# Two attention layers over four images in float32: the last image's output projection by seven half products

## The chip, the cores and the metric

The kernel runs on one core of a Trainium2 chip. The metric is the time of one execution on the device in microseconds, as the median of several runs. A separate execution was recorded by the hardware profiler; all names of engines below are the profile's: PE is TensorE's matmuls and PEld its weight loads, DVE is VectorE, ACT is ScalarE, POOL is GpSimd, and SP is SyncE, which here only issues transfers. An engine carries out its instructions in the order in which the program emitted them.

## The reference

The input x has 4 images of 32 x 32 positions with 768 channels, all in float32. Two layers follow one another. Each layer normalises x over 32 groups of channels, computes attention with 12 heads of 64 channels over the 1024 positions of an image, with a bias from relative positions in the scores, projects the result and adds it to x:

```
x = x + attention_0(groupnorm(x)) @ Wproj_0 + bproj_0
x = x + attention_1(groupnorm(x)) @ Wproj_1.T + bproj_1
attention: softmax(scale * q k^T + rel_h + rel_w) v,   q, k, v = projections of groupnorm(x)
```

The change is in the last line's projection, for the last image of the second layer: an output of 768 channels by 1024 positions from the attention's 768 channels.

## The kernel before

**Units of work.** A layer of one input image is called an image here: images 0 to 3 are layer 0, 4 to 7 layer 1; image 7 is the last (`LAST`). An image has six pairs of heads (`pair` 0 to 5, each 128 channels), a pair has eight units (`n` 0 to 7, each 128 query positions). One loop (L1005) goes over all 384 units, and its body writes the order of the instructions of every engine out by hand, a unit at a time, under a manual schedule. In each unit the body emits: transfers and other things due at the start; two bias additions on GpSimd for the unit after next (`biases`, L528); the score matmuls of the next unit (`scores`, L543); their softmax up to the exponentials on VectorE and ScalarE (`exponentials`, L556); the transposes of this unit's weights on VectorE and their store to DRAM (`turn`, L578: td<-tb), read back later in another layout (`read_back`, L587: pt<-td); the reciprocal on VectorE and the two divisions on ScalarE for the next unit (`divide`, L571); sums on GpSimd that are due; and then pieces of projections. At n = 6 and n = 2 it emits the attention-times-values matmuls (`weigh`, L598), 64 instructions, whose result VectorE evicts from PSUM into `attn` tiles (L622).

**The bias from positions.** For each pair, part of the bias goes through DRAM: ScalarE stores it (tdr<-t), and four transfers on SP read it back along diagonals (rel<-tdr, L521). The bias additions of units 4 to 7 wait for the second set.

**Projections by seven products.** The products of a pair (q, k, v) and the output projections of images 0 to 6 are computed by a scheme of the Strassen-Winograd kind: the matrices are split in two along the contracted channels, the outputs and the positions, and seven products of halves with some sums replace eight. For the output projection these are called a (two products), b (two), c (two) and d (one), for o = 0, 1, 2, each with contracted pairs 0 to 2 in one half and 3 to 5 in the other (`out_product`, L711). The differences of weights that they need are made beforehand by GpSimd and kept in DRAM tables (`combined`, L628; `single`, L650: for layer 1, in images 3 and 4). The sums of attention tiles are made on GpSimd (`out_sums`, L698). VectorE evicts the products. Kind a needs pairs 0 to 2 alone and runs in pairs 4 and 5 of the image; b, c and d need the others too and run in pairs 0 to 3 of the next image.

**The last image** has no next one. Its projection is plain (`project_out_two`, L821; `project_out`, L829; `put_result`, L842): for each of 6 output chunks and 2 halves of positions, six contracted pairs, in the three parts that `CUTS` (L624) tells: pairs 0 to 2, pairs 3 and 4, pair 5. That is 72 matmuls of 128 x 128 by 128 x 512. The first part for outputs 0 and 1 runs in pair 4 and at the start of pair 5 in the form called crossed: matmuls of 64 rows, two at a time on the two halves of the array, the product begun in one unit and finished in a later one. The rest is a list `todo`, from which `take` (L900) emits as many matmuls at the end of each unit of the last pair as `shares` tells: 3, 6, 0, 6, 6, 6, 0, 6, then 24. After that come the last attention-times-values matmuls and the last six products (L1137).

**Evictions and buffers.** Products go to PSUM tiles of the pool `ps_m`, which has two buffers (L79); attention-times-values and the position matmuls use the same two. A product begins when the tile before last has been evicted. The eviction of a product is emitted with its last matmul, that is behind that unit's transposes, reciprocal and divisions. `put_result` adds the first part to the residual and the output's bias on VectorE (L846), the other parts to that sum (L849). The residual halves and the weights are loaded by `fetch` (L792) and `fetch_last` (L808) on SP's queue. Most 128 x 512 tiles come from one pool of 35 shared buffers (`unit`, L89, `UNITS`, L54).

Of the kernel before, what the change touches and what calls it, by code (L numbers as in the profile page):

```python
# [57 lines left out]
def attention_blocks(ctx: ExitStack, tc: tile.TileContext, a: dict, out: bass.AP):  # L58
# [539 lines left out]
    def weigh(g, quarters):  # L598

        if quarters[0] % 2 == 0:
            attn_of.setdefault(g, []).append(unit(f"attn_{g}_{quarters[0] // 2}"))
        n = len(quarters)
        av = ps_m.tile([P, S], FP, tag="m", name=f"av_{g}_{quarters[0]}")[:, : n * 2 * P]
        for at, quarter in enumerate(quarters):
            for k in range(NT):
                for h in range(2):
                    rows = slice(h * D, (h + 1) * D)  # L610
                    nc.tensor.matmul(  # L611
                        av[rows, at * 2 * P : (at + 1) * 2 * P], lhsT=v_of[g][:, k, rows],
                        rhs=pt_of[g, quarter].rearrange("p n r k h i -> p (n r) k h i")[:, :, k, h, :],
                        start=(k == 0), stop=(k == NT - 1),
                    )
        at = quarters[0] % 2 * 2 * P
        to = attn_of[g][quarters[0] // 2][:, at : at + n * 2 * P]
        im, pair = divmod(g, NP)
        if images[im][0] == 0:
            nc.vector.tensor_copy(to, av)  # L620
        else:
            nc.vector.tensor_scalar(to, av, bqkv[:, 2, pair : pair + 1], None, ALU.add)  # L622

    CUTS = [0, NC // 2, NC - 1, NC]  # L624
    LAST = NI - 1
    tables = {}
# [23 lines left out]
    def single(l, o, which):  # L650

        if (l, o) not in tables:
            tables[l, o] = dram.tile([4, P, NB * P], FP, tag=f"tw{l}_{o}", name=f"tw_{l}_{o}")
        raw = lambda k: a[f"wo{l}"][o + k % 2 * NB][:, k // 2 * NB * P : (k // 2 + 1) * NB * P]
        made = lambda k: tables[l, o][k - 1]
        x, y = (unit(f"t{k}_{l}_{o}_{which}")[:, : NB * P] for k in range(2))
        for to, at in zip((x, y), {
            1: lambda: (raw(1), raw(0)), 2: lambda: (raw(3), made(1)),
            4: lambda: (raw(2), made(2)), 3: lambda: (raw(3), raw(1)),
        }[which]()):  # L660
            nc.sync.dma_start(out=to, in_=at)
        at_sums.setdefault(here[0] + 2, []).append(
            lambda: nc.gpsimd.tensor_tensor(x, x, y, ALU.subtract)
        )
        at_start.setdefault(here[0] + 3, []).append(
            lambda: nc.sync.dma_start(out=made(which), in_=x)
        )
# [9 lines left out]
    def fetch_out(at):  # L677

        if at >= len(order):
            if at < len(order) + 2:  # L680
                fetch(3 + 4 * (at - len(order)))
            return
# [13 lines left out]
    s3_of, kept_x, kept_y = {}, {}, {}  # L696

    def out_sums(im, which, c):  # L698

        part = lambda k, i: attn_of[im * NP + k * NB + c][i]  # L700
        if which == 3:
            s3_of[im, c] = unit(f"os3_{im}_{c}")
        to, x, y, op = {
            3: lambda: (s3_of[im, c], part(0, 0), part(0, 1), ALU.subtract),
            1: lambda: (part(0, 1), part(0, 1), part(1, 1), ALU.add),
            2: lambda: (part(0, 0), part(0, 1), part(0, 0), ALU.subtract),
            4: lambda: (part(1, 0), part(1, 0), part(0, 0), ALU.subtract),
        }[which]()
        nc.gpsimd.tensor_tensor(to, x, y, op)

    def out_product(im, kind, o):  # L711
        l = images[im][0]
        ws = out_weights[im, kind, o]
        half = lambda p, i: [attn_of[im * NP + p * NB + c][i] for c in range(NB)]
        t = ps_m.tile([P, 2, HALF], FP, tag="m", name=f"o{kind}_{im}_{o}")
        if kind == "d":
            for c in range(NB):
                for h, rows in enumerate(ROWS):
                    nc.tensor.matmul(  # L719
                        t[:, h, :], lhsT=ws[0][rows, c, :], rhs=half(1, 0)[c][rows],  # L720
                        start=(c == 0), stop=(c == NB - 1),
                    )
        else:
            xs = {
                "a": lambda: (half(0, 0), [s3_of[im, c] for c in range(NB)]),
                "b": lambda: (half(1, 0), half(0, 0)),
                "c": lambda: (half(0, 1), half(1, 1)),
            }[kind]()
            yield from crossed(t, range(NB), lambda t, c, h, rows: (
                t[:, h, :], ws[h][rows, c, :], xs[h][c][rows]  # L730
            ))
        t0, t1 = t[:, 0, :], t[:, 1, :]
# [5 lines left out]
        if kind == "a":  # L738
            kept_x[o], kept_y[o] = unit(f"ox_{im}_{o}"), unit(f"oy_{im}_{o}")
            nc.vector.tensor_copy(kept_x[o], t0)  # L740
            add(kept_y[o], t1, kept_x[o])
        elif kind == "b":
# [3 lines left out]
            add(y, t1, y)  # L746
# [8 lines left out]
        else:  # L755
            x = kept_x[o]
            with_bias(x, t0, x, o + NB)
            add(x, t1, x)
            complete(im, o + NB, 0, x, (3, 6, 14)[o])
        at = order_of[im, kind, o]  # L760
        ahead_by = {"d0": (2, 3), "c2": (3,), "d1": (), "d2": (2,)}
        for k in ahead_by.get(f"{kind}{o}", (2,)):
            early.append(lambda k=k: fetch_out(at + k))

    def complete(im, o, i, r, delay):
        l, b = images[im]
        if im + 1 == LAST and delay > 4:
            delay = 2
# [19 lines left out]
    parts = [(o, i) for o in range(NC) for i in range(2)]  # L788
    res_of, sum_of = {}, {}
    fetched = [0, 0]  # L790

    def fetch(upto):  # L792

        l, b = images[LAST]
        while fetched[0] <= min(upto, len(parts) - 1):
            o, i = parts[fetched[0]]
            if i == 0:
                w = wopool.tile([P, NB, P], FP, tag="wo", name=f"wo_{LAST}_{o}")
                nc.sync.dma_start(
                    out=w, in_=a[f"wo{l}"][o][:, : NB * P].rearrange("p (c o) -> p c o", o=P)  # L800
                )
                for c in range(NB):
                    wo_of[LAST, o, c] = w[:, c, :]
            res_of[o, i] = unit(f"res_{LAST}_{o}_{i}")
            load_half(res_of[o, i], l, b, o, i)
            fetched[0] += 1

    def fetch_last():  # L808
# [3 lines left out]
        for c in range(NC // 2, NC):  # L812
            if c + 1 < NC:
                w = weights_of(NPAIR, "ac"[c - NC // 2])
# [6 lines left out]
    def project_out_two(o):  # L821
        t = ps_m.tile([P, 2, HALF], FP, tag="m", name=f"oo_{o}")
        yield from crossed(t, range(NB), lambda t, c, i, rows: (
            t[:, i, :], wo_of[LAST, o, c][rows], attn_of[LAST * NP + c][i][rows],
        ))
        for i in range(2):
            put_result(0, o, i, t[:, i, :])

    def project_out(p, o, i):  # L829
        c0, c1 = CUTS[p : p + 2]  # L830
        t = ps_m.tile([P, S], FP, tag="m", name=f"o_{p}_{o}_{i}")[:, :HALF]
        for c in range(c0, c1):
            nc.tensor.matmul(  # L833
                t, lhsT=wo_of[LAST, o, c], rhs=attn_of[LAST * NP + c][i],
                start=(c == c0), stop=(c == c1 - 1),
            )
            if c < c1 - 1:
                yield True
        put_result(p, o, i, t)
        yield True  # L840

    def put_result(p, o, i, t):  # L842
        l, b = images[LAST]
        if p == 0:
            sum_of[o, i] = to = res_of[o, i]
            nc.vector.scalar_tensor_tensor(to, t, bo[l][:, o : o + 1], to, ALU.add, ALU.add)  # L846
        else:
            to = sum_of[o, i]
            nc.vector.tensor_tensor(to, t, to, ALU.add)  # L849
        if p == 2:  # L850
            nc.sync.dma_start(out=chunk(dsts[l][b], o)[:, i * HALF : (i + 1) * HALF], in_=to)
        if p == 0 and i == 1:
            fetch(2 * o + 9)
# [24 lines left out]
    def out_groups(g):  # L878
# [3 lines left out]
        if im == LAST and pair >= 4:  # L882
            make = [lambda o=o: project_out_two(o) for o in range(2)] if pair == 4 else [None, None]
        else:
            at = im if pair >= 4 else im - 1
            if at < 0:
                return {}
            make = [
                (lambda name=name: out_product(at, name[0], int(name[1]))) if name else None
                for name in plan if name is not None  # L890
            ]
# [5 lines left out]
    def put_out(p, groups):  # L897
        return [(project_out(p, at // 2, at % 2), CUTS[p + 1] - CUTS[p]) for at in groups]
# [27 lines left out]
    for k in range(NB):  # L926
        for stage, after in enumerate((0, 4, 5, 6)):
            combining.setdefault(NT * k + after, []).append((0, k, stage))
    singles = [(0, 3), (1, 3), (2, 3), (0, 1), (0, 2), (0, 4), (1, 1), (1, 2), (2, 1), (2, 2), (1, 4), (2, 4)]
    singles = {  # L930
        ((3 + k // 6) * NP + p) * NT + n: made
        for k, (made, (p, n)) in enumerate(zip(singles, 2 * [(0, 1), (0, 4), (1, 2), (2, 4), (3, 2), (4, 0)]))
# [15 lines left out]
    with tc.manual_schedule(engines=ENGINES):  # L948
# [56 lines left out]
        for at, (g, n) in enumerate(units):  # L1005
# [3 lines left out]
            if n == 0:  # L1009
# [10 lines left out]
                if g + 1 == NPAIR:  # L1020
                    fetch_last()
                    todo = put_out(0, range(4, 12)) + put_out(1, range(12))
                    todo += put_out(2, range(0, 12, 2))
# [81 lines left out]
            if not end:  # L1105
                for which, c in sum_steps.get((pair, n), ()):
                    sums(im + 1, which, c)
            if (pair, n) in out_sum_steps:
# [17 lines left out]
            take(todo, shares[n])  # L1126
            if n == 6:
# [9 lines left out]
        todo = put_out(2, range(1, 12, 2))  # L1137
# [56 lines left out]
```

## Time and profile before

| | us |
|---|---|
| median of three runs | 3244.69 |
| lowest, highest | 3243.01, 3245.06 |
| profiled execution, its own time | 3248.18 |
| its span, first to last instruction | 3246.2 |
| images 1 to 6, from first score matmul to first score matmul | 398.8 to 400.3 |
| last pair, scores of unit 1 to the last attention-times-values matmuls | 3155.56 to 3229.05 |

Times in the profile count from the span's first instruction. A float32 matmul appears as two instructions. Matmuls overlap in the array, so that starts, not durations, tell their pace. In a timeline, equal instructions that follow one another are one line (x12 is twelve of them), and the bracket at its end tells how long the engine was idle before it and what ended that. A row of the groups gives the line, the engine, what is written from what, the number of instructions, their busy time and the mean ns of one, and then the idle time before them.

### The profile page before, as it was taken

Reading aid. Unit: us, or ns where it says so; the run is one execution under the profiler, and the core shown is the slowest. Engines: PE = TensorE matmul, PEld = TensorE weight load, DVE = VectorE, ACT = ScalarE, POOL = GpSimd, SP = SyncE. Lnnn points to the kernel's source line nnn. Section 1 sums busy time; section 2 is a strip of 40 time slices with the busy share of each in tenths; the row PEclk is TensorE's granted clock in tenths of the full one; section 3 lists DMA queues with packets and bytes.
Section 4 is the critical chain, followed back from the end, with each engine's and each line's share of the span. In section 5 each row is a group of like instructions: output and inputs, shape, how many; then the busy total and the mean of one; then the engine's idle time right before and its main releaser. Section 6 shows DMA issues by size and latency. Waiting matters only on the chain.

```text
span 3246.2 us, 63998 instructions
## 1 busy us (share of the span) xinstructions
PE 3216.8 (99%) x24800; PEld 1855.4 (57%) x24800; DVE 2578.6 (79%) x4085; ACT 2093.2 (64%) x3098; POOL 2571.3 (79%) x1364
## 2 busy tenths in 40 slices
PE   8999999999999999999999999999999999999999
PEld 5565555555565555555565555555565555555554
DVE  7888878887888877788777887778777788787785
ACT  5677766666566665667656676666766567665662
POOL 6888967789777897878978889777897778977762
PEclk9999999999999999999999999999999999999999
DMA  5998888999989998899988999789988899888996
GB/s 196 339 340 320 311 310 313 323 338 327 319 303 330 342 328 317 296 346 343 324 308 309 342 338 339 284 302 335 325 325 302 298 340 330 312 311 303 322 337 252
DMA packets 386847, 1028.84 MB, mean 317 GB/s; under 512 B 31344, under 2 KB 73200, under 8 KB 337392
## 3 DMA queue, kind: packets, MB, share of 16 engines
q1 hardware_dynamic: 370992, 997.33, 86.2%
q10 hardware_dynamic: 15552, 27.43, 2.3%
q8 instruction: 196, 3.21, 0.4%
q14 instruction: 107, 0.88, 0.1%
HBM read 566.93 MB, written 457.70 MB: 316 GB/s over the span
## 4 chain that ended last, share of the span: by engine, by line
PE 94%; DVE 3%; DMA 2%; issue 1%; ACT 0%; POOL 0%; SPq 0%; DVEq 0%; POOLq 0%
PE pj L357 22%; PE av L611 20%; PE s L550 20%; PE pv L357 11%; PE pj L385 4%; PE oa L357 3%; PE ob L357 3%; PE oc L357 3%; PE tp L488 2%; PE pv L441 2%; PE od L719 2%; PE o L833 1%; DMA td<-tb 1%; DVE tb L582 1%; DMA pt<-td 1%
## 5 line engine op out<-in xcount | busy, mean ns | idle before, releaser
L536 POOL TENSOR_TENSOR sc<-rel 128x1024 f32<-128x1024 f32 x768 | 1943.6, 2557 | 537.8 <-DVE tb L582 416.0
L576 ACT ACTIVATE sc<-sc,sm 128x1024 f32<-128x1024 f32 x768 | 841.1, 1143 | 595.0 <-DVE sm L573 481.3
L562 DVE CUSTOM_DVE_ANT_0 sc<-s,sc 128x1024 f32<-128x1024 f32 x768 | 911.3, 1226 | 337.5 <-PE s L550 323.5
L566 ACT ACTIVATE sc<-sc,sm 128x1024 f32<-128x1024 f32 x768 | 877.2, 1144 | 255.7 <-DVE sm L562 253.2
L582 DVE STREAM_TRANSPOSE tb<-sc 128x1024 f32<-128x1024 f32 x768 | 912.4, 1233 | 18.3 <-DMA td<-tb 17.1
L550 PE MATMUL s<-k,q 64*128 64x512 f32 x3072 | 736.4, 596 | 0.5 <-DVE k L401 0.5
L611 PE MATMUL av<-pt,v 128*64 128x256 f32 x6144 | 684.9, 381 | 5.1 <-DMA pt<-td 5.1
L611 PEld LDWEIGHTS av<-pt,v 128*64 128x64 f32 x6144 | 433.7, 137 | 285.5 <-issue 42.8
L550 PEld LDWEIGHTS s<-k,q 64*128 64x128 f32 x3072 | 285.0, 187 | 296.6 <-issue 264.3
L357 PEld LDWEIGHTS pv<-wv,xn 64*128 64x128 f32 x4608 | 271.3, 188 | 35.1 <-issue 28.9
L357 PE MATMUL pv<-wv,xn 64*128 64x128 f32 x4608 | 273.8, 272 | 0.5 <-DVE wv L346 0.5
L357 PE MATMUL pj<-xn,wa 64*128 64x512 f32 x1152 | 265.6, 593 | 4.2 <-DVE wa L346 2.6
L357 PE MATMUL pj<-xn,w 64*128 64x512 f32 x1152 | 263.2, 589 | 0.0
L357 PE MATMUL pj<-s,w 64*128 64x512 f32 x576 | 262.9, 590 | 0.0
L357 PE MATMUL pj<-s,wc 64*128 64x512 f32 x576 | 262.9, 590 | 0.0
L357 PEld LDWEIGHTS pj<-xn,wa 64*128 64x128 f32 x1152 | 111.0, 187 | 140.9 <-issue 115.5
L357 PEld LDWEIGHTS pj<-xn,w 64*128 64x128 f32 x1152 | 111.7, 187 | 135.5 <-issue 133.1
L459 DVE TENSOR_TENSOR v<-pv,v 128x512 f32<-128x512 f32 x216 | 140.2, 686 | 57.9 <-ACT v L461 40.9
L493 ACT COPY t<-tp 128x512 f32<-128x512 f32 x96 | 56.1, 585 | 160.6 <-PE tp L488 160.6
L511 ACT COPY rel<-raw 32x256 f32<-32x256 f32 x384 | 154.8, 403 | 3.6
L357 PEld LDWEIGHTS pv<-wv,s 64*128 64x128 f32 x2304 | 137.1, 188 | 24.2 <-issue 16.9
L357 PEld LDWEIGHTS pj<-s,wc 64*128 64x128 f32 x576 | 105.6, 187 | 68.6 <-issue 64.8
(134 smaller groups left out, 3395.8 us busy)
## 6 DMA issues: line engine op xcount, KB each, us to landing
td<-tb SPq DMA_DIRECT2D x384, 1024.0 KB, 5.3
pt<-td SPq DMA_DIRECT2D x382, 1024.0 KB, 8.3
tdr<-t ACTq DMA_DIRECT2D x96, 256.0 KB, 5.4
wa<-in_wqk SPq DMA_DIRECT2D x48, 384.0 KB, 4.2
wc<-in_wqk SPq DMA_DIRECT2D x48, 384.0 KB, 5.6
wv<-in_wv SPq DMA_DIRECT2D x24, 768.0 KB, 11.8
xn<-in_x SPq DMA_DIRECT2D x48, 256.0 KB, 5.4
res<-in_x SPq DMA_DIRECT2D x48, 256.0 KB, 5.7
```

The lines of the kernel that those rows point to most:

```text
L357: nc.tensor.matmul(to, lhsT=w, rhs=x, start=at == half == 0, stop=at == 0 and half == 1)
L385: nc.tensor.matmul(t[:, h, :], lhsT=w[rows, c, :], rhs=x[c][rows, :], start=(c == 0), stop=(c == NB - 1),)
L441: nc.tensor.matmul(t[:, h, b, :], lhsT=s4[c][rows, b * P : (b + 1) * P], rhs=w22[rows, c, :], start=(b, c) == (0, 0), stop=(b, c) == (3, N ...
L459: add = lambda to, x, y: nc.vector.tensor_tensor(to, x, y, ALU.add)
L511: nc.scalar.copy(rel[rows], raw[rows, :, :, WIDE - 1 - HW - y : WIDE - 1 - y])
L536: nc.gpsimd.tensor_tensor(sc.rearrange("p (a k) (u l) -> p a (k u) l", a=4, l=8), rel[:, h, m, :].unsqueeze(1).unsqueeze(3).to_broadcast(s ...
L550: nc.tensor.matmul(ps[h][:, cols], lhsT=q[rows, n * P : (n + 1) * P], rhs=k[rows, cols], start=True, stop=True,)
L562: nc.vector.tensor_tensor_reduce(out=sc, in0=ps[h], in1=sc, scale=-scale, scalar=BIG, op0=ALU.add, op1=ALU.min, accum_out=st[:, 0, h : h + 1],
L566: nc.scalar.activation(sc, sc, AF.Exp, bias=st[:, 0, h : h + 1], scale=-1.0, accum_out=st[:, 1, h : h + 1],)
L576: nc.scalar.mul(sc, sc, st[:, 2, h : h + 1])
L582: nc.vector.transpose(tb[:, :, h, :], sc_of[g, n, h])
L611: nc.tensor.matmul(av[rows, at * 2 * P : (at + 1) * 2 * P], lhsT=v_of[g][:, k, rows], rhs=pt_of[g, quarter].rearrange("p n r k h i -> p (n ...
```

## The change

For the last image, pairs 0 to 3 are projected by seven half products as in the other images, with two pairs in each half (`width` is 2 in place of 3); pairs 4 and 5 are added afterwards in the plain form, each on its own.

- a0 and a1 run in crossed form where the plain products of outputs 0 and 1 ran. The other products (a2, b0 to b2, c0, c1, d0, d1, c2, d2) are at the head of `todo`, as full matmuls of 128 rows, four for a, b and c and two for d (`last_product`); then come twelve products of one matmul each for pair 4, and six for pair 5. The shares are as before.
- Both results of an a are copied out of PSUM by ScalarE; the sum that VectorE made there is now made by GpSimd when b is evicted. The residual is added by GpSimd (`add_last`, a unit later where there is one), and pairs 4 and 5 are added to that by VectorE.
- `weigh` evicts the first values of the last pair (pair 5's unit 6) on ScalarE in place of VectorE.
- The differences of weights for two pairs are made in images 5 and 6, as those for three pairs are in images 3 and 4: twelve times two loads, a GpSimd subtraction and a store.
- Sums of attention tiles run on GpSimd in pair 4 (`last_sums`), one a unit, and two at once in unit 4 of pair 5.
- Weights of the products are loaded into shared buffers, two transfers of 128 KB each, from unit 2 of pair 4 on (`last_fetches`); the residual halves in units 1 to 6 of the last pair, two a unit (`load_last`); `fetch_last` loads two weight tiles in place of three.

```diff
+        if g + 1 == NPAIR and n == 2:
+            nc.scalar.activation(to, av, AF.Identity, bias=bqkv[:, 2, pair : pair + 1])
+        elif images[im][0] == 0:
...
+    width = lambda im: NB if im < LAST else NB - 1
...
+    last_order = ("a0", "a1", "a2", "b0", "b1", "b2", "c0", "c1", "d0", "d1", "c2", "d2")
...
+    def last_product(kind, o):
+        ws, xs = out_operands(LAST, kind, o)
+        n = width(LAST)
+        t = ps_m.tile([P, 2, HALF], FP, tag="m", name=f"o{kind}_{LAST}_{o}")
+        for h, (w, x) in enumerate(zip(ws, xs)):
+            for c in range(n):
+                nc.tensor.matmul(
+                    t[:, h, :], lhsT=w[:, c, :], rhs=x[c], start=(c == 0), stop=(c == n - 1)
+                )
+                if (h, c) < (len(ws) - 1, n - 1):
+                    yield True
+        out_results(LAST, kind, o, t, [t[:, h, :] for h in range(len(ws))])
+        yield True
...
         if kind == "a":
             kept_x[o], kept_y[o] = unit(f"ox_{im}_{o}"), unit(f"oy_{im}_{o}")
+            if im == LAST:
+                nc.scalar.copy(kept_x[o], t0)
+                nc.scalar.copy(kept_y[o], t1)
+                return
             nc.vector.tensor_copy(kept_x[o], t0)
             add(kept_y[o], t1, kept_x[o])
         elif kind == "b":
             x, y, r = kept_x[o], kept_y[o], unit(f"or_{im}_{o}_0")
             with_bias(r, t0, x, o)
             add(x, t1, x)
-            add(y, t1, y)
+            if im == LAST:
+                nc.gpsimd.tensor_tensor(y, y, x, ALU.add)
+            else:
+                add(y, t1, y)
...
+            if len(ts) == 2:
+                add(x, t1, x)
...
     def complete(im, o, i, r, delay):
         l, b = images[im]
+        if im == LAST:
+            sum_of[o, i] = r
+            add_last = lambda: nc.gpsimd.tensor_tensor(r, r, res_of[o, i], ALU.add)
+            if here[0] + 1 < len(units):
+                at_sums.setdefault(here[0] + 1, []).append(add_last)
+            else:
+                add_last()
+            return
...
+    def project_out(c, o, i):
+        t = ps_m.tile([P, S], FP, tag="m", name=f"o_{c}_{o}_{i}")[:, :HALF]
+        nc.tensor.matmul(
+            t, lhsT=wo_of[LAST, o, c], rhs=attn_of[LAST * NP + c][i], start=True, stop=True
+        )
+        to = sum_of[o, i]
+        nc.vector.tensor_tensor(to, t, to, ALU.add)
...
-                    todo = put_out(0, range(4, 12)) + put_out(1, range(12))
-                    todo += put_out(2, range(0, 12, 2))
+                    todo = [(last_product(kind, o), 2 if kind == "d" else 4) for kind, o in last_order[2:]]
+                    todo += put_out(NC - 2, range(12)) + put_out(NC - 1, range(0, 12, 2))
+            if end and (pair, n) in last_fetches:
+                fetch_last_out(last_fetches[pair, n])
+            if g + 1 == NPAIR and 0 < n < NT - 1:
+                for o, i in res_order[2 * n - 2 : 2 * n]:
+                    load_last(o, i)
...
+            if end and (pair, n) == (5, 4):
+                for c in range(width(LAST)):
+                    out_sums(LAST, 4, c)
...
-        todo = put_out(2, range(1, 12, 2))
+        todo = put_out(NC - 1, range(1, 12, 2))
```

## The prediction

> **What bounds the kernel.** I read the busy shares first, then the chain of waits.
>
> ```profile
> PE 3216.8 (99%) x24800; PEld 1855.4 (57%) x24800; DVE 2578.6 (79%) x4085; ACT 2093.2 (64%) x3098; POOL 2571.3 (79%) x1364
> ...
> PE 94%; DVE 3%; DMA 2%; issue 1%; ACT 0%; POOL 0%; SPq 0%; DVEq 0%; POOLq 0%
> ```
>
> TensorE is the bound: a matmul taken out is time taken out, unless TensorE then waits. Where it waits already is told by its timeline in the last pair (start, us, instructions, in brackets the idle time and its releaser):
>
> ```profile
> 3173.72 5.42 PE L833 MATMUL o<-attn,wo 128*128 128x512 f32 x12
> 3179.07 1.99 PE L550 MATMUL s<-k,q 64*128 64x512 f32 x8
> 3180.98 5.42 PE L833 MATMUL o<-attn,wo 128*128 128x512 f32 x12
> 3186.33 1.99 PE L550 MATMUL s<-k,q 64*128 64x512 f32 x8
> ...
> 3193.87 1.13 PE L833 MATMUL o<-attn,wa 128*128 128x512 f32 x2 [1.06 <-DVE res L846]
> ...
> 3207.68 1.12 PE L833 MATMUL o<-attn,wa 128*128 128x512 f32 x2 [0.87 <-DVE res L849]
> 3208.64 1.02 PE L833 MATMUL o<-attn,wc 128*128 128x512 f32 x2
> ...
> 3223.23 5.89 PE L833 MATMUL o<-attn,w_last 128*128 128x512 f32 x12
> ```
>
> A unit of the last pair is its score matmuls and six projection matmuls, 7.26 us (3179.07 to 3186.33). A full matmul is two instructions, 0.858 us apart (3208.64 to 3222.37, sixteen). The two waits are the key to the change. Products take turns in two PSUM buffers. Before, a unit holds two products of three matmuls, one for each buffer. Only where a third product begins in a unit does TensorE wait for an eviction. When evictions run is seen on VectorE and ScalarE, here in the unit whose scores start at 3155.56:
>
> ```profile
> 3157.69 1.23 DVE L562 CUSTOM_DVE_ANT_0 sc<-s,sc 128x1024 f32<-128x1024 f32 x1 [0.40 <-PE s L550]
> 3159.98 2.37 DVE L582 STREAM_TRANSPOSE tb<-sc 128x1024 f32<-128x1024 f32 x2
> 3162.27 0.12 DVE L573 RECIPROCAL sm<-sm 128x2 f32<-128x2 f32 x1
> 3162.32 1.39 DVE L846 SCALAR_TENSOR_TENSOR res<-o,bo,res 128x512 f32<-128x512 f32 x2
> 3162.43 2.19 ACT L576 ACTIVATE sc<-sc,sm 128x1024 f32<-128x1024 f32 x2 [1.09 <-DVE sm L573]
> ```
>
> Evictions are emitted behind the unit's softmax step, transposes and reciprocal: VectorE reaches them 6.76 us after the scores start, and ScalarE, behind its two divisions, 9.06 us after (3162.43 + 2.19 - 3155.56).
>
> **Removed matmuls.** Pair 4: the four blocks of 12 half instructions (oo) become blocks of 8. Twelve are 2.58 us in the chain, so 4 x 0.86 = -3.4 us. Nothing waits there before. The two copies of a0 and a1 stand before the divisions on ScalarE, which idles 1.66 and 2.42 us there. Last pair: 60 matmuls become 58, -1.7. Six of 72 in all: -5.1 us.
>
> **Products of four against unchanged shares (3, 6, 0, 6, 6, 6, 0, 6).** Worked unit by unit from the offsets above.
> Unit 1 runs a2's last matmul, four of b0, one of b1. b1 needs a2's buffer, whose two copies on ScalarE come behind the divisions: 9.06 + two copies. The nearest row, L409, evicts the same shape in 0.580; with overlap I take 1.1. TensorE could start b1 at 1.92 + 5 x 0.858 = 6.2 and starts at 10.15: a wait of 3.95. The unit takes 11.0, +3.75. Bounds: if b1 got b0's buffer it would wait for VectorE, to 6.76 + 1.4 = 8.2, +1.9; and if copies cost L306's 0.80 each, +4.2. I take +3.75, since the wait of 1.06 above ended with the older buffer's eviction.
> Unit 4: b2's last, c0, one of c1. c1 waits for b2's two evictions, 6.76 + 1.4 = 8.2, instead of 6.2: unit 9.1, +1.85.
> Unit 5: three of c1, two of d0, one of d1. d1 waits for c1's three evictions (0.69 + 0.75 + 0.75, less overlap), 6.76 + 2.1 = 8.9: unit 9.8 against 8.59 (which held the 1.06), +1.2.
> Units 2, 3, 6 keep their lengths: at most two buffers change hands.
> Tail, 3203.90 to 3229.05: two matmuls less -1.7, the 0.87 gone, the wait for c2's three evictions before pair 4's first product +0.65, ScalarE's eviction of the last pair's first values +0.15. Pair 4's twelve products now have one matmul each. For such products the w_last row shows 0.953 each (VectorE starts at 3223.43, 3225.34: 1.91 for two), so 12 x 0.095 = +1.15. Sum -0.6.
> What is late after each wait is the next unit's scores, and with them that unit's whole softmax; the transfers that are due there (pt, rel, td) gain the same time.
> Together 3.75 + 1.85 + 1.2 - 0.6 = +6.2 us in the last pair (its two matmuls included), against -3.4 in pair 4: +2.8.
>
> **The clock.** A wait of 4 us is new for TensorE in this stage, and the windows of the trace show what idling does (us, then PE, PEld, DVE, ACT, POOL busy, granted clock, DMA share, GB/s):
>
> ```profile
> 3155.00:3230.00 75.00, 73.07 (x290) 32.12 (x290) 51.00 (x75) 29.70 (x38) 25.15 (x10) 1.00 0.83 294
> 3230.00:3240.00 10.00, 9.41 (x65) 5.12 (x62) 2.51 (x5) 0.00 (x0) 0.00 (x0) 1.00 0.17 62
> 3240.00:3246.20 6.20, 2.56 (x6) 0.59 (x4) 2.60 (x4) 0.00 (x0) 0.00 (x0) 0.89 0.60 221
> ```
>
> The last matmul ends at 3242.56 (3236.76 + 5.80); a mean clock of 0.89 over 6.20 us is half speed for 1.4 us, from 3244.8: the clock fell 2.2 us after the last matmul. Waits of 1.06 left it at 1.00. The Trainium skill ("TensorE: Matmul & The Clock Gate", Part 1) says that the clock halves after an idle window of about 3.4 us in a free-running grid and needs about 3.4 us of work to come back. By the rule only unit 1's wait can cover a window, by (3.95 - 3.41) / 3.41 = 16%: 0.3 us. By the row a window about two thirds idle is enough: unit 1's wait nearly always holds one, unit 5's (d1 ready at 5.9, started at 8.9: 3.0) mostly, unit 4's (2.0) sometimes. Each closing costs 3.4 us at half speed, 1.7 us (an estimate from that page). I weigh them 1, 0.75 and 0.35: 2.1 x 1.7 = +3.6. I take the row; the sum is +6.7 by it and +3.4 by the rule.
>
> **Other edits.** Twelve more weight differences in images 5 and 6, each two loads, one GpSimd subtraction and a store. Images 3 and 4 have them already: their pair 3 has one score-to-score step of 9.66 and 9.61 us where images 5 and 6 have 9.44. +0.15 to 0.2 an image, +0.3 in all.
> GpSimd: 8 sums, 3 "y + x" and 12 residual adds. It is idle 10.7 us in the last pair before its last eight bias adds. Of them the fourth unit's waits for rel until 3171.35; between that and the last bias come six new operations of 1.285 us (L709), 7.7 us. It then ends about 1 to 3 us ahead of unit 7's softmax step: hidden, 0. Without that cover each us late costs one, since softmax, division and ScalarE's eviction follow.
> SP: fetch_last falls from three transfers of 384 KB to two. The residual loads, in pairs 4 and 5 before, go into units 1 to 6 of the last pair, two in each, beside two 128 KB loads of weights. They stand ahead of that unit's td store and pt read, and of the four rel loads in unit 1. At 0.4 us an issue this is under 2 us a unit. TensorE reads the last pt at about 3232.8 and the store before it was issued at 3207.07, so several us cover it: 0. Transfers into the 35 shared buffers could wait for a slot: I count at most 34 live.
> VectorE: 42 operations for the last image's projection in place of 36, and one eviction less. Those of pair 4 fall away (the copies are ScalarE's); the last pair has eight more at about 0.72 us, less the eviction. What they hold up is in the waits above; the two units with attention-times-values matmuls, 8.98 us long, let VectorE catch up. The moved eviction of the last pair's first values lets the last transposes start without waiting for it (3204.02 to 3204.68 before): 0.7 us earlier, off TensorE's path, 0.
> The six sums in pair 4 (1.285 each, one a unit) stand behind two bias adds of 5.1 us in units of 7 us or more, and a0 asks for them two units later: 0.
>
> **Sum.** -3.4 + 6.2 + 3.6 + 0.3 = +6.7 us: span 3246.2 to 3252.9, its own time 3248.18 to 3254.9. The profiled execution stands 3.5 us over the median of the runs; applied to the median 3244.69: **3251.4 us**, +0.21%.
>
> **Rivals.**
> 1. Likeliest, as above, 0.50. Own range 3248 to 3255; the clock's windows decide which side of 0.2%.
> 2. The waits without the clock, 0.14: +3.1, 3247.8. For it: the page's full window. Against: the row at 3244.8.
> 3. On the other side: the waits don't come, 0.12. Place: b1's start in unit 1. If the copies ran before the divisions (at 1.92 + 0.86 + 1.1 = 3.9 us), the buffers would be free when asked for; it decides once copies end before 6.2. Then -5.1 - 1.06 - 0.87 + 1.15 + 0.3 = -5.6, 3239.1. The Trainium skill ("TensorEngine Tiling (Array Packing)", PSUM Bottleneck) speaks for it: share PSUM's evacuation between ScalarE and VectorE. The row of L576, 2.19 us of divisions ahead of the copies, speaks against it.
> 4. GpSimd or SP becomes a second bound in the last pair, 0.24: "y + x" waits for VectorE's evictions and keeps the next bias adds behind it. It decides when the last bias ends over 1 to 3 us late; with 4 us beyond that, +10.7, 3255.4. For it: bias adds take 20.10 us of 3171.35 to 3191.45 without a gap. Against: they run two units ahead.
>
> **How the numbers follow.** 0.2% is 6.5 us, about what a measurement of this kernel can tell from no change. Slower: 0.32 of case 1 and all of 4, 0.56. Faster: 0.08, from case 3's far end. Same: 0.18 + 0.14 + 0.04 = 0.36. Range 3242 to 3258: it leaves out most of case 3 below and the far end of 4 above.
>
> **What will show it.** In unit 1 of the last pair an idle stretch of TensorE of about 4 us ended by ScalarE's copy of oa; about 2 and 3 us in units 4 and 5 ended by VectorE; a granted clock under 1.00 there; pair 4 shorter by 3.4 us; w_last's pace in pair 4's products. I am wrong if b1 starts within 1 us of b0's end, if the clock stays at 1.00 (then case 2), or if TensorE waits for pt, rel or a bias.

## The result, and the profile after

The changed kernel takes 3255.89 us as a median of six runs (3251.72 to 3261.33), the kernel before 3245.44 in six runs on the same chip (3243.01 to 3248.51): a ratio of 1.003, interval 1.002 to 1.004, 10.5 us longer. Two later pairs of medians gave 1.0022 (1.0012 to 1.0033) and 1.0022 (1.0016 to 1.0029), 8.4 and 8.0 us. Forecast were 3251.4 us and +6.7.

The page of the kernel after, its totals and the summary of its chain, hardly differs from that of before:

```profile
span 3251.8 us, 64136 instructions
...
PE 3218.2 (99%) x24780; PEld 1852.2 (57%) x24780; DVE 2582.0 (79%) x4090; ACT 2096.4 (64%) x3105; POOL 2607.4 (80%) x1399
...
PE 94%; DVE 3%; DMA 1%; issue 1%; ACT 0%; POOL 0%; SPq 0%; DVEq 0%; POOLq 0%
```

TensorE has 20 instructions less and is busy 1.4 us more. A busy sum that rises while work is taken out is what a lower clock looks like from this view; it doesn't tell where. Two other views do. First, what TensorE waits for, in a window of after from 2400 us to the end, its three largest rows (us in total, times, longest):

```profile
PE ob L778 <- ACT oy L798: 3.6, 1, 3.6
PE od L778 <- DVE oy L792: 2.4, 1, 2.4
PE oc L778 <- DVE ox L789: 1.8, 1, 1.8
```

Three new waits, where the prediction put them. TensorE's timeline of the last pair shows each in its unit (start, us, instructions, in brackets the wait and its releaser):

```profile
3148.84 1.99 PE L550 MATMUL s<-k,q 64*128 64x512 f32 x8
...
3151.72 1.88 PE L778 MATMUL ob<-attn,wb 128*128 128x512 f32 x4
3153.44 1.88 PE L778 MATMUL ob<-os,wb 128*128 128x512 f32 x4
3158.91 2.08 PE L778 MATMUL ob<-attn,wb 128*128 128x512 f32 x2 [3.59 <-ACT oy L798]
3160.92 3.76 PE L550 MATMUL s<-k,q 64*128 64x512 f32 x8
3164.61 7.13 PE L611 MATMUL av<-pt,v 128*64 128x256 f32 x64
3171.67 1.99 PE L550 MATMUL s<-k,q 64*128 64x512 f32 x8
...
3187.20 1.13 PE L778 MATMUL oc<-attn,wc 128*128 128x512 f32 x2 [1.79 <-DVE ox L789]
3188.25 3.66 PE L550 MATMUL s<-k,q 64*128 64x512 f32 x8
...
3198.84 2.08 PE L778 MATMUL od<-attn,wd 128*128 128x512 f32 x2 [2.44 <-DVE oy L792]
3200.85 2.58 PE L550 MATMUL s<-k,q 64*128 64x512 f32 x8
```

Unit 1 starts at 3148.84; its third product (b1) can't begin before a2's buffer has been copied out, 10.07 us later. a2's last matmul ran from 3150.76 to 3151.88, 7 us before that. The two copies out of its buffer (ox, oy) stand behind the unit's divisions, as ScalarE's timeline of after shows:

```profile
3155.71 2.19 ACT L576 ACTIVATE sc<-sc,sm 128x1024 f32<-128x1024 f32 x2 [0.83 <-DVE sm L573]
3157.81 0.56 ACT L797 COPY ox<-oa 128x512 f32<-128x512 f32 x1
3158.28 0.58 ACT L798 COPY oy<-oa 128x512 f32<-128x512 f32 x1
```

Beside the waits, the eight score instructions behind each take 3.76, 3.66 and 2.58 us where the undisturbed ones at 3148.84 and 3171.67 take 1.99. The second view is the row of windows of the same execution (us, then PE, PEld, DVE, ACT, POOL busy, granted clock, DMA share, GB/s):

```profile
3150.80:3160.90 10.10, 6.51 (x14) 2.27 (x12) 6.05 (x9) 7.22 (x10) 3.77 (x2) 0.84 1.08 381
3160.90:3171.70 10.80, 10.80 (x75) 5.73 (x74) 4.71 (x7) 4.52 (x6) 6.01 (x3) 0.83 0.92 329
3171.70:3188.00 16.30, 14.51 (x42) 5.65 (x40) 13.71 (x21) 9.20 (x13) 13.33 (x8) 1.00 1.01 355
3188.00:3192.00 4.00, 4.00 (x10) 1.24 (x10) 1.15 (x2) 0.00 (x0) 4.00 (x4) 0.57 0.86 240
3192.00:3203.00 11.00, 8.56 (x20) 3.16 (x20) 7.36 (x11) 4.58 (x6) 11.00 (x8) 0.84 0.92 343
3203.00:3248.00 45.00, 43.90 (x192) 18.83 (x190) 27.34 (x39) 5.27 (x7) 5.45 (x5) 1.00 0.55 195
```

The clock falls behind each of the three waits, and nowhere else in the last pair. Multiplying each row's length by the clock it lacks gives 1.6 + 1.8 + 1.7 + 1.8 = 6.9 us of TensorE's clock. Some of it fell into the waits themselves, so that the kernel lost less (below).

**How lengths are compared below.** From first score matmul to first score matmul, images 1 to 6 together took 2396.7 to 2399.6 us in every profiled execution of every kernel. Image 0 took 354.3 to 363.4, the kernel before included. After's happened to be 5 us shorter than before's, so that its span grew by only 5.6 us. I therefore compare the **last image**, from its first score matmul to the end of the span. It took 443.2 us before and 452.1, 449.3 and 453.6 in three executions of the changed kernel: 8.5 us more in the mean, close to the medians' differences.

The steps of the last pair, in us from one unit's first score matmul to the next (projections of unit n come after the scores of unit n + 1, so that the step of unit 1 begins with the scores of unit 2, at 3155.56 in before; the prediction counts in the same way):

| | unit 7 of pair 4 | 0 | 1 | 2 | 3 | 4 | 5 | 6 to the end |
|---|---|---|---|---|---|---|---|---|
| before | 7.86 | 7.16 | 7.26 | 8.98 | 7.26 | 7.26 | 8.59 | 51.3 |
| changed | 6.15 | 6.30 | 12.07 | 10.75 | 7.26 | 9.32 | 12.60 | 51.0 |
| changed, filled with idle work | 6.15 | 6.30 | 11.12 | 8.97 | 7.26 | 9.32 | 9.98 | 50.4 |
| changed, aligned | 6.15 | 7.16 | 8.98 | 8.98 | 8.98 | 7.81 | 7.26 | 46.9 |

The last two rows are experiments.

### The profile page after: what moved, and what is told of

It is laid out like the page before. It is cut to its first block, busy times and chain, and to the rows that moved or that the text cites. A ratio compares the mean times of both kernels' runs of the same rounds, so it can differ in the third digit from the quotient of the medians.

```text
span 3251.8 us, 64136 instructions
## 1 busy us (share of the span) xinstructions
PE 3218.2 (99%) x24780; PEld 1852.2 (57%) x24780; DVE 2582.0 (79%) x4090; ACT 2096.4 (64%) x3105; POOL 2607.4 (80%) x1399
## 4 chain that ended last, share of the span: by engine, by line
PE 94%; DVE 3%; DMA 1%; issue 1%; ACT 0%; POOL 0%; SPq 0%; DVEq 0%; POOLq 0%
PE pj L357 22%; PE av L611 20%; PE s L550 20%; PE pv L357 11%; PE pj L385 4%; PE oa L357 3%; PE ob L357 3%; PE oc L357 3%; PE tp L488 2%; PE pv L441 2%; PE od L756 2%; DVE tb L582 1%; DMA td<-tb 1%; PE o L882 1%; DVE sc L562 0%
```

## Experiments

My theory: third products that begin within one unit wait for evictions behind softmax work (+2.8 us net), and the waits halve the clock (+3.6). The rivals to be told from it: waits alone; the engine of the eviction, not its place; GpSimd or SP as a second bound; and another of the change's edits as the cause.

### The changed kernel again

As given, in two groups of runs, to stand beside the experiments on the same chip.

> The changed kernel once more, beside the others on one chip. Theory A (waits for evictions, and the clock that they let close): about 10 us over the kernel before, with runs spread over several us because the grid of the clock's windows starts elsewhere in each execution. Theory B (waits alone): the waits are the same in every execution, so the spread is that of the kernel before, 2 to 5 us.

> The changed kernel, beside the same with copies by VectorE and beside the two aligned ones on one chip. Theory A: 8 to 10 us over the kernel before; one to three closings of the clock in the last pair of the profiled execution, always one in unit 1.

Measured: 3255.73 beside 3247.36, and 3254.06 beside 3246.05. The three waits were 3.59, 1.79 and 2.44 or 2.45 us in both. The clock was not the same. In the first execution only unit 1's wait was followed by a lower clock (a mean of 0.85 and 0.83 in the two rows there); here are its waits in units 4 and 5 in the timeline of TensorE:

```profile
3192.78 1.12 PE L778 MATMUL oc<-attn,wc 128*128 128x512 f32 x2 [1.79 <-DVE ox L789]
...
3202.76 1.12 PE L778 MATMUL od<-attn,wd 128*128 128x512 f32 x2 [2.44 <-DVE oy L792]
```

and the windows of the same execution around them:

```profile
3194.00:3198.00 4.00, 4.00 (x13) 1.58 (x14) 2.79 (x4) 0.77 (x1) 4.00 (x4) 1.00 0.99 346
3198.00:3210.00 12.00, 9.55 (x56) 4.64 (x56) 9.38 (x15) 6.19 (x10) 11.11 (x8) 1.00 0.72 266
```

Equal waits, clock 1.00. The spread of the runs, which was to tell the two theories apart, does so only on one chip: 13.6 us against 6.4 of the kernel before in the second group, but 10.4 against 10.6 in the first. The record of the clock tells them apart. The last image of this execution is 449.3 us, 2.8 and 4.3 shorter than in the other two. What the waits cost is fixed by the schedule, what the clock costs is not.

### Waits kept, TensorE kept busy in them

Eight full matmuls are added at the head of b0, c0 and d0. Their result is discarded by the first matmul of the product, which starts the sum anew. Nothing of the computation is left out.

```diff
     def last_product(kind, o):
...
+        for _ in range({"b0": 3, "c0": 2, "d0": 3}.get(f"{kind}{o}", 0)):
+            nc.tensor.matmul(t[:, 0, :], lhsT=ws[0][:, 0, :], rhs=xs[0][0], start=True, stop=True)
```

> TensorE gets eight matmuls more: b0, c0 and d0 begin with 3, 2 and 3 matmuls whose result is thrown away, in the three stretches of the last pair where it waits. The evictions that b1, c1 and d1 wait for are not moved. Theory A: no closing of the clock in the last pair, waits of about 1.0, 0.3 and 0.4 us left, units of 11.0, 9.1 and 9.8 us; 5 to 6 us faster than the changed kernel, some 3 to 4 us over the kernel before. Theory B: the time of the changed kernel within 1 us, since the waits end when they did. If TensorE's work as such were the bound: 6.9 us slower than the changed kernel.

Measured: 3249.0 us, 1.0005 of before (0.9997 to 1.0013), and 6.7 us under the changed kernel on the same chip. Work was added and the kernel became faster. TensorE's timeline of unit 1 in this kernel:

```profile
3151.08 2.74 PE L777 MATMUL ob<-attn,wb 128*128 128x512 f32 x6
...
3158.26 1.13 PE L780 MATMUL ob<-attn,wb 128*128 128x512 f32 x2 [1.01 <-ACT oy L800]
3159.32 1.99 PE L550 MATMUL s<-k,q 64*128 64x512 f32 x8
```

b1 still starts on ScalarE's copy, some 10 us into the unit; three matmuls (L777) fill 2.57 us of what was idle. Its windows, unit 1 and then the stretch with units 4 and 5 and the tail:

```profile
3150.11:3159.30 9.19, 8.18 (x20) 3.25 (x18) 6.15 (x9) 7.27 (x10) 3.01 (x3) 1.00 1.09 378
...
3184.00:3241.00 57.00, 55.90 (x226) 23.58 (x226) 36.29 (x53) 10.45 (x14) 21.19 (x16) 1.00 0.67 246
```

The clock is 1.00 in these rows and in those between. The last image is 446.2 us, 3.0 more than before: this is the price of the waits alone, net of the matmuls saved, and what is above it in the changed kernel, 5.9, 3.1 and 7.5 us, is the clock's. The rival of waits without the clock falls for the changed kernel, and is true for this one.

### a2 kept whole in one unit

The shares of the first two units, so that a2 is done in unit 0 and no third product begins in unit 1. Units 4 and 5 stay misaligned.

```diff
-            shares = [3, 6, 0, 6, 6, 6, 0, 6]
+            shares = [4, 5, 0, 6, 6, 6, 0, 6]
```

> Shares 4, 5 in place of 3, 6: a2 ends in unit 0, so that its two copies stand behind the divisions of the unit before. Only the wait in unit 1 goes. Theory A: unit 1 falls from 12.1 to about 6.3 us and unit 2 from 10.8 to 9.0, unit 0 grows by 0.9: some 6 us faster than the changed kernel, 3 to 5 over the kernel before. Theory B: 3.6 us faster. A rival, by which added transfers or GpSimd work set the last pair's pace: no change, the time turns up as another wait.

Measured: 3249.49, 6.2 us under the changed kernel. Unit 1's wait is gone, and the other two remain, unit 4's 0.8 us longer, here in this kernel's timeline of TensorE:

```profile
3189.18 1.12 PE L778 MATMUL oc<-attn,wc 128*128 128x512 f32 x2 [2.56 <-DVE ox L789]
...
3200.76 2.08 PE L778 MATMUL od<-attn,wd 128*128 128x512 f32 x2 [2.40 <-DVE oy L792]
```

The clock fell behind both in this execution. Unit 1's wait with its clock is worth 6.2 of the 8.4 us by which the changed kernel was longer on this chip.

### Products aligned with the units

No unit holds parts of more than two products: a2 in unit 0, b0 and b1 in unit 1, b2 and c0 in unit 3, c1 and d0 in unit 4, d1 and c2 in unit 5, d2 and the first matmul for pair 4 in the tail. The operands that this asks for earlier (two sums, and the loads of the weights) move one unit ahead.

```diff
-            shares = [3, 6, 0, 6, 6, 6, 0, 6]
+            shares = [4, 8, 0, 8, 6, 6, 0, 3]
...
-            if end and (pair, n) == (5, 4):
+            if end and (pair, n) == (5, 3):
...
-        last_fetches[divmod(4 * NT + 3 + k, NT)] = k
+        last_fetches[divmod(4 * NT + 2 + k, NT)] = k
```

> Shares 4, 8, 0, 8, 6, 6, 0, 3: no unit begins a third product. The two last sums on GpSimd come one unit earlier, and so do the loads of the products' weights. Theory A: no wait over 0.5 us before the last values, the clock stays at 1.00, 15 us faster than the changed kernel and 5 to 6 us faster than the kernel before (5.1 us of matmuls and 1.9 us of waits less, 1.2 us more for products of one matmul). Rival, GpSimd or transfers as a second bound: waits for a bias, for rel, pt or weights appear, and the time stays at or over that of the kernel before.

> Aligned shares again, on the same chip as the next one. Theory A: 5 to 8 us faster than the kernel before, 14 to 17 faster than the changed kernel.

Measured: 3239.3 (0.9973 of before, 0.9962 to 0.9984) and on another chip 3240.88 (0.9984, 0.9976 to 0.9993), 16.4 and 13.2 us under the changed kernel (the second a little short of the 14 to 17 forecast). Last image 438.9 and 439.1, 4.3 and 4.1 under before. TensorE's timeline of unit 1 when aligned:

```profile
3149.29 1.99 PE L550 MATMUL s<-k,q 64*128 64x512 f32 x8
3151.21 1.98 PE L778 MATMUL ob<-attn,wb 128*128 128x512 f32 x4
3153.03 1.88 PE L778 MATMUL ob<-os,wb 128*128 128x512 f32 x4
3154.75 1.88 PE L778 MATMUL ob<-attn,wb 128*128 128x512 f32 x4
3156.47 1.88 PE L778 MATMUL ob<-os,wb 128*128 128x512 f32 x4
3158.28 1.99 PE L550 MATMUL s<-k,q 64*128 64x512 f32 x8
```

Eight matmuls without a gap, in a unit of 8.98 us where six took 12.07. The longest wait of TensorE in this execution, from 3100 us on:

```profile
PE o L882 <- ACT attn L620: 0.8, 1, 0.8
```

All other edits of the change are in this kernel: GpSimd's sums, the copies on ScalarE, the added loads and weight differences (two of the sums, and the loads of the products' weights, a unit earlier). None of them makes a loss by itself; the next run shows that the copies on ScalarE lengthen a wait where products and units don't fit. This version is faster than both kernels.

### The copies of a on VectorE

```diff
-                nc.scalar.copy(kept_x[o], t0)
-                nc.scalar.copy(kept_y[o], t1)
+                nc.vector.tensor_copy(kept_x[o], t0)
+                nc.vector.tensor_copy(kept_y[o], t1)
```

> The changed kernel with one part undone: both results of a0, a1 and a2 are copied out of PSUM by VectorE, not ScalarE. Theory A: b1 waits for VectorE behind the reciprocal in place of ScalarE behind the divisions, 2.0 us in place of 3.6; unit 1 is 9.1 to 9.5 us long, the clock closes there in some executions only; 2 to 4 us faster than the changed kernel. Rival: VectorE was too full, so that two copies more in the last pair hold its transposes up: no faster than the changed kernel.

> As before, copies of a0, a1 and a2 by VectorE, now on the same chip as the changed kernel. Theory A: unit 1 is 9.1 us and without a closing of the clock in most executions, 3 to 6 us faster than the changed kernel. If the 7 us between two chips were the copies' own: 6 to 8 us.

Measured: 3248.12 (1.0007, 0.9998 to 1.0015) and 3249.75 (1.0011, 1.0002 to 1.0019), the second 4.3 under the changed kernel on its chip. Unit 1's wait in the first, by TensorE's timeline, is not gone but shorter, and 9.13 us became its length in both:

```profile
3160.52 1.12 PE L778 MATMUL ob<-attn,wb 128*128 128x512 f32 x2 [1.60 <-DVE oy L798]
```

So the wait has two parts. 1.60 us comes from a third product in the unit, with evictions behind the transposes; 2.0 more comes from the copies' standing behind ScalarE's divisions. (That copies ahead of the divisions would do away with the wait was not tried.) The clock stayed at 1.00 behind this wait in both executions; a later wait lowered it once in each.

### Alignment, with the last pair's first values on VectorE, or "y + x" on VectorE

Each is the aligned kernel with one part of the change undone.

```diff
-        if g + 1 == NPAIR and n == 2:
-            nc.scalar.activation(to, av, AF.Identity, bias=bqkv[:, 2, pair : pair + 1])
-        elif images[im][0] == 0:
+        if images[im][0] == 0:
```

> The kernel with aligned shares, and the last pair's first values evicted by VectorE as before the change. The prediction called this part nothing. Theory A: the wait of 0.8 us for ScalarE's eviction goes, the last transposes come 0.7 us later behind cover: 0 to 0.8 us faster than with aligned shares alone. Rival: the part carries the last transposes forward and with them the last read-back: slower by 1 us or more.

> Aligned shares and the last pair's first values by VectorE, on the same chip. Theory A, from the two profiles' last images (438.9 and 438.0 us): 0.5 to 1 us faster than with aligned shares alone, which the runs can't tell from nothing; a difference of 2 us or more either way would be against it.

Measured: 3240.84 (0.9983 of before, 0.9977 to 0.999) in one group of runs, last image 438.0, and in a second group 3241.76 (0.9986, 0.9979 to 0.9993) beside 3240.88 for the aligned kernel on the same chip, last image 439.2 beside 439.1. The small gain that was forecast did not show; the moved eviction can't be told from nothing.

```diff
-                nc.gpsimd.tensor_tensor(y, y, x, ALU.add)
+                add(y, y, x)
```

> The kernel with aligned shares, and the sum of y and x at b made by VectorE in place of GpSimd. Theory A: GpSimd is no bound, VectorE has 0.7 us more three times, at the end of units in which it is ahead: within 0.5 us of the kernel with aligned shares. Rival: the sum on GpSimd keeps the next bias additions behind it: 1 to 3 us faster without it.

Measured: 3241.09 (0.9982 of before, 0.9975 to 0.9988). The aligned kernel did not run in this group; in the later one, on the same chip, it took 3240.88 (0.9984), so that the medians show no difference. The profiled execution was the slowest of the 21 (3245.88), and it shows what I had not expected. VectorE's timeline in this kernel, and below it GpSimd's bias add at the same place:

```profile
3179.09 0.69 DVE L789 TENSOR_TENSOR ox<-ob,ox 128x512 f32<-128x512 f32 x1
3179.82 3.01 DVE L789 TENSOR_TENSOR oy<-oy,ox 128x512 f32<-128x512 f32 x1
```

```profile
3179.75 2.53 POOL L536 TENSOR_TENSOR sc<-rel 128x1024 f32<-128x1024 f32 x1
```

The sum of two tiles in SBUF took 3.01 us and ended 0.55 us after GpSimd's bias add, which had started 0.07 us before it; the two earlier sums of this kind, with no bias add beside them, took 0.69. VectorE then had no gap for 11 us, and d1, two units on, found its buffer 1.94 us late, as TensorE's timeline has it:

```profile
3191.57 2.87 PE L778 MATMUL od<-attn,wd 128*128 128x512 f32 x4 [1.94 <-DVE oy L792]
```

The clock fell there too; the last image was 440.7, 1.7 over the aligned kernel's mean. So in this execution the sum on VectorE was followed by a wait that the aligned kernel's profiles don't have. That the one made the other is argued from the order of the two timelines, and that the sum on GpSimd pays is not shown, since the medians are equal.

### The kernel before, shifted against its units

None of the change: only the shares, so that in four units a third product begins.

```diff
-            shares = [3, 6, 0, 6, 6, 6, 0, 6]
+            shares = [2, 6, 0, 6, 6, 6, 0, 7]
```

> The kernel before with nothing of the change but its list of products shifted by one matmul against the units: shares 2, 6, 0, 6, 6, 6, 0, 7. Work, evictions and transfers stay. Theory A: units 1, 3, 4 and 5 now begin a third product, each waits about 2 us for the eviction behind the unit's reciprocal (9.3 us in place of 7.26; unit 5 from 8.6 to 9.3), 6 to 7 us, and the clock may close: 6.5 to 10 us slower than the kernel before. Rival: the change's evictions (three for c), its GpSimd work and its transfers make the waits, not where products begin: within 1 us of the kernel before.

Measured: 3253.27 beside 3246.57, ratio 1.0021 (1.0013 to 1.003), 6.7 us. Its waits and one of them in TensorE's timeline:

```profile
PE o L833 <- DVE res L846: 7.7, 4, 1.9
```

```profile
3153.81 3.70 PE L833 MATMUL o<-attn,wo 128*128 128x512 f32 x8
3159.43 1.98 PE L833 MATMUL o<-attn,wo 128*128 128x512 f32 x4 [1.92 <-DVE res L846]
```

A loss of most of the change's size (6.7 of 8 to 10 us), made in the kernel before by moving the products' boundaries by one matmul. Here the clock stayed up in the profiled execution, and the last image is 449.8, 6.6 over before: its four waits of 1.92 are 7.7, and the two waits of before, 1.06 and 0.87, are gone.

## Why the prediction was right, point by point

The time lies in the range, slower by more than 0.2% as the larger chance had it, and by the likeliest mechanism; but at the median 0.9 us above that case's own range. The rival whose number is nearest, 3255.4 with GpSimd or SP as a second bound, is not what happened. That the median lies in the range is in part luck: the range reached up to 3258 for the sake of that rival, and the likeliest case by itself ended at 3255.

**Pair 4, -3.4.** Right: the two steps with one block of 8 in place of 12 (7.16 to 6.30 in the table, and 6.87 to 6.01 ahead of it) and the step with two such blocks (7.86 to 6.15) are 0.86, 0.86 and 1.71 us shorter, 3.43.

**Unit 1, +3.75.** Right: +3.86, from the filled kernel's 11.12. The place of the eviction was worked out as 9.06 us and two copies after the unit's scores. The copies began at 8.97 and b1 at 10.07 (forecast 10.15). The wait was 3.59, not 3.95, because TensorE ended its five matmuls later than the sum had it, at the same end of the unit. The lower bound that was not taken, VectorE's buffer, +1.9, is what the copies on VectorE measured: 9.13 - 7.26.

**Units 4 and 5, +1.85 and +1.2.** Right: +2.06 and +1.39, without the clock. Waits of 1.79 and 2.44 for 2.0 and 3.0.

**Tail and the rest, -0.6.** -0.9 (51.3 to 50.4), with pair 4's twelve products at 0.965 us each (3217.20 to 3228.78) where 0.953 was taken from the row of w_last. The sum of all this is +3.0 where +2.8 was forecast.

**The clock, +3.6.** Mechanism right, size too small: this is the mis-sized term. Its mean is 5.5 us in three executions (5.9, 3.1, 7.5). I had counted 2.1 stretches of 3.4 us at half speed. The record of the clock shows four, two and five, 3.7 in the mean: units 4 and 5 each lowered it in two executions of three (weighed 0.35 and 0.75), and unit 1's lowered clock lasted two stretches in every one of the three, where I had counted one. A stretch cost 1.5 us in the mean (5.5 / 3.7), not 1.7: in after, TensorE was still waiting in the first 1.2 us of unit 1's lowered clock (3157.69 to 3158.91). The choice between row and rule decided this. The Trainium skill ("TensorE: Matmul & The Clock Gate", Part 1) asks for an idle window of 3.4 us, which would have forbidden units 4 and 5 altogether and most of unit 1. The row of before, a clock that fell 2.2 us after the last matmul, said less is enough. The measurement decides against the page's rule. The three stretches of 3.41 us that ended as the clock fell, in after:

```profile
3154.28:3157.69 3.41, 1.04 (x3) 0.19 (x1) 2.74 (x5) 2.58 (x4) 0.56 (x1) 1.00 1.05 389
3185.00:3188.41 3.41, 1.62 (x5) 0.46 (x6) 3.37 (x6) 2.19 (x2) 3.41 (x3) 1.00 1.10 347
3195.24:3198.65 3.41, 1.16 (x3) 0.19 (x1) 3.37 (x6) 2.32 (x4) 3.41 (x4) 1.00 0.88 347
```

TensorE was busy for 30, 48 and 34% of them. And three in the execution with the last image of 449.3 us, around waits of the same length, on the same spacing of 3.413 us counted from the one fall of the clock in its last pair, at whose end the clock stayed up:

```profile
3191.14:3194.55 3.41, 1.77 (x6) 0.78 (x8) 3.34 (x7) 2.19 (x2) 3.41 (x4) 1.00 0.99 334
...
3197.97:3201.38 3.41, 2.34 (x6) 0.76 (x4) 3.41 (x7) 2.32 (x5) 3.41 (x2) 1.00 1.00 395
3201.38:3204.79 3.41, 2.03 (x8) 0.80 (x10) 1.95 (x3) 1.51 (x2) 3.41 (x4) 1.00 1.00 338
```

Busy for 52, 69 and 59%: here the wait of 2.44 us lay across a boundary, and neither side was half idle; of the wait of 1.79 us some 0.15 us fell ahead of its window.

**Weight differences, +0.3.** Wrong by its whole size, but small: images 5 and 6 took 398.78 and 398.80 us after, 398.78 each before. The row behind it was no constant: the step of image 4 that was 9.61 in before is 9.44 in after, with the same weight differences in it.

**Costed at nothing.** GpSimd, SP and the transfers: right, TensorE never waits for a bias, rel or pt in the last pair, and the rival of a second bound did not occur. The moved eviction: right, unmeasurable. VectorE's own work: right in the change as made; with "y + x" on VectorE as well, one execution had a wait of 1.94 us, and the medians show no loss.

**The other side.** The rival in which the waits don't come named unit 1's third product as the place where it is decided. The aligned kernel decided it there, and came out at -4.3 and -4.1 in the last image, -8.1 and -5.2 in the medians, where -5.6 was worked out. The Trainium skill's advice ("TensorEngine Tiling (Array Packing)", PSUM Bottleneck) to share evictions between the two engines did not decide it: with the copies on ScalarE the wait was 3.59, on VectorE 1.60, and with products aligned, the copies on ScalarE again, none. Sharing hurt where the copies stood behind ScalarE's divisions and did no harm where nothing waited for them.

## What to carry to other kernels

When products are made smaller, their boundaries move against the units into which the schedule is cut: count how many products *begin* in a unit, and compare it with the number of buffers that are free by then, before counting matmuls. An eviction is released by its place in its engine's queue, so a less loaded engine can be the later one. And price a wait of TensorE twice, once as time and once as the half-speed stretch that follows when it leaves about half of a 3.413 us window of the clock idle (more on this below).

## What the runs showed that I had not expected

- **Discarded work paid.** Eight added matmuls made the changed kernel 6.7 us faster, by holding the clock at 1.00 through the three waits.
- **Half a window is enough.** In the record of the clock, the time between two changes is a whole multiple of 3.413 us: in the last pair of after 6.83, 23.89, 3.41, 6.83 and 3.41, from the fall at 3157.69 on. With the executions cut into windows on this grid, those windows that ended in a fall of the clock behind a wait were less than half busy (0.03 to 0.48 over all profiled executions), none above 0.50 ended so, and some between 0.40 and 0.49 did not. What decides between 0.40 and 0.50 is open. The position of the windows against the program differs from execution to execution, and one schedule cost 3.1 to 7.5 us of clock.
- **A lowered clock lasts 3.41 or 6.83 us.** In the last pair of the changed kernel it lasted 3.41 where the wait had ended 1.1 to 1.2 us before the clock fell, or ended 0.2 us after, and 6.83 where it ended 0.3 to 1.4 us after, as unit 1's did each time. These are seven falls; a rule is not shown by them.
- **VectorE held by GpSimd.** A VectorE sum of two SBUF tiles took 3.01 us in place of 0.69 beside a GpSimd add. The Trainium skill states this ("SBUF — State Buffer", Who interferes with whom): such an instruction shares a port with GpSimd, and the second to issue is blocked until the first is done. The run agrees: the bias add started first (3179.75 against 3179.82), and the sum ended 0.55 us after it did, nearly its own length of 0.69.
